# Cross-attention on one core: another hand-written order for the same 2281 operations, 127 of them on another engine

## The chip, the cores and the metric

The kernel runs on one core of a Trainium2 chip. A core has five engines with a queue of instructions each: TensorE (PE, matrix products), VectorE (DVE), ScalarE (ACT), GpSimd (POOL) and SyncE (SP, which only starts transfers). An engine works through its own queue strictly in order; an instruction waits on semaphores that other engines and transfers raise. Sixteen DMA engines move data between HBM and the on-chip memory (SBUF). The metric is the device time of one execution in microseconds (us); lower is better.

## The reference, cut to what matters

```python
# x (2, 2048, 640), ctx (2, 128, 384); H = 640, 8 heads of 80; T = 4 adapter tokens
enc, ca = ctx[:, :124], ctx[:, 124:]
query = x @ Wq
hs    = mha(query, enc @ Wk, enc @ Wv)            # 2048 x 124 scores per head
ca_q1 = einsum('btc,th->bch', ca, Wq_ca)[:, linspace(0, 383, 2048).astype(int)]
ca_hs1 = mha(ca_q1, x, x)                         # 384 distinct rows x 2048 keys per head
ca_hs2 = mha(ca_hs1 @ Wq, ca @ Wk_ca, ca @ Wv_ca) # 2048 x 4 scores per head
out = (hs + ca_hs2) @ Wout + b_out + x
```

All data is 32-bit float. The 2048 rows of `ca_q1` hold only 384 different ones, so the second attention is worked out for 384 rows and spread to the output rows at the end by indirect transfers that add.

## The kernel before, in words

**Stages.** The image rows of the two batch elements are cut into tiles of 128 rows (`xz`, `xi`, `x_more`, `last_rows` are buffers of such rows) and into 16 units of 256 rows (numbers 0 to 15 in names like `sc_5_0`, `po_15_1`). At the start the kernel loads x and the weights and turns them with TensorE transposes (`pt_x`, `pt_wq`, `pt_ctx`). `pq` products make the queries; `s`, `ea`, `acc` are scores, exponentials and sums of the adapter attention over the image (DVE takes a maximum `mx` of each block of scores, ACT the exponential `ea`, PE sums it into `acc`); `sc`, `m`, `p`, `eb`, `pT`, `ph` are scores, maxima, exponentials, transposed probabilities and results of the text attention; `po` is the product with Wout, whose pieces DVE adds to `x_more` or `last_rows`, whence they are stored. GpSimd adds the adapter's share `o` with one indirect transfer for a 128-row tile (line 2351).

**What sets the order.** The program is written by a small planner, the class `Desk`. Each stage is a Python generator that yields operations (`Do`); an operation has a set of engines that may run it. `Desk.run` (line 351) takes, of all operations that are ready to be written, the one with the lowest number in the table `TURNS` (line 85), and that number modulo six names the engine (PE, ACT, DVE, POOL, SP, or none). So `TURNS` alone fixes both the order of every queue and which engine does a copy, a sum or a store; each instruction is pinned in that order (`pin`, line 378). Lines 396, 405 and 410 issue the matrix products and transposes, line 427 all operations of DVE, ACT and POOL, line 447 the plain transfers, line 1363 a second kind of transfer for `xi`.

**Transfers.** ACT starts the loads of Wq, SP nearly all others, and both start stores. Wq comes in five chunks: two whole ones, two in halves of 64 rows, the fifth in five pieces of 16 or 32 rows (`chunk` and `last` in `first_loads`, line 667). The same generator then issues, on SP, four tiles `xz` of x, `wqca_sb`, `ctx_sb`, and the weights `w_kca` and `w_k` (128 partitions x 3 x 640 words, 983 KB each):

```python
yield Do("SP", lambda: dma(ctx_sb, enc.rearrange("b t c -> t b c"), 1.6), [], marks=["ctx"])
kca = yield load_w("kca", Wk_ca, after=[])
k = yield load_w("k", Wk, after=[])
```

In the built program the transfers of SP and ACT share eight completion semaphores, `DMAHW0` to `DMAHW7`, and a transfer that takes one of them first waits until the transfer that had it before has landed. The planner's own model has eight open transfers for each engine (`SLOTS`, line 74, `transfer`, line 450).

Of the kernel before, what the change touches and what calls it, by code (L numbers as in the profile page):

```python
# [65 lines left out]
class Desk:  # L66
# [19 lines left out]
        ".1": [995], ".2": [44, 59, 60, 84, 96, 108, 114, 120, 126, 132, 150, 174, 198, 210, 234, 978], ".3": [608],  # L86
        ".4": [5, 52, 76, 82, 94, 106, 352, 412, 442], ".4.1": [37, 67, 169, 241, 265], ".5": [468, 499, 534, 547,
        558, 584, 590], ".6": [11, 17, 144, 162, 204, 222, 258, 294, 300, 329], ".6.1": [140], ".6.2": [188],
        ".6.3": [218], ".6.4": [284], ".6.5": [157], ".6.6": [194], ".6.7": [229], ".6.8": [253], ".6.9": [278],
        ".6.10": [314], ".6.11": [319], ".7": [290, 510, 530, 1058], ".8": [23, 29, 35, 180, 246, 270, 306, 360,  # L90
        384, 396, 420, 426, 456, 486, 540, 576, 636, 726, 792, 803], ".8.1": [404], ".8.2": [416], ".8.3": [518],
        ".8.4": [703], ".8.5": [935, 1003, 1064, 1069, 1334], ".8.5.1": [1174], ".8.5.2": [1258], ".8.5.3": [1301],
        ".8.5.4": [1307, 1372, 1529, 1531, 1541, 1597], ".8.5.5": [1426], ".8.5.6": [1414], ".8.5.7": [1481],
        ".8.5.8": [1619, 1660, 1781, 1783, 1937, 1975], ".9": [368, 377, 450, 474, 485, 522, 564, 575, 618, 624,
        635, 672, 708, 762, 786], ".9.1": [464], ".9.2": [493], ".9.3": [553], ".9.4": [596], ".9.5": [643], ".9.6":
        [650], ".9.7": [685], ".9.8": [770], ".9.9": [812], ".9.10": [817], ".10": [605, 678, 716, 734, 828, 848,
        858, 919, 926, 936, 950, 972, 1088], ".11": [656, 744, 834, 912, 942, 960, 1025, 1031, 1039, 1052, 1084,
        1168, 1264, 1360, 1408, 1471], ".11.1": [782], ".11.2": [872], ".11.3": [956], ".11.4": [968], ".11.5":
        [1016], ".12": [1103, 1113, 1364], ".13": [760, 778, 1270], ".14": [724, 1176, 1214, 1308, 1328, 1416, 1441,
        1446, 1465, 1490, 1642, 1834, 1870, 1948, 2782, 4306, 5614, 6568], ".15": [694, 699, 984, 1032, 1242, 1272,  # L100
        1343], ".15.1": [1076], ".15.2": [1094], ".15.3": [1279], ".15.4": [1315], ".16": [1509], ".17": [335, 1104,
        1141, 1147, 1157, 1160, 1183, 1196, 1220, 1285, 1352], ".17.1": [1544, 1588, 1592, 1612, 1715, 1721, 2596,
        2830, 3832, 4780], ".18": [341, 1139], ".19": [809, 2663], ".20": [346, 358, 382, 394, 436, 448, 508, 616,
        664, 671, 752, 824, 842, 854, 866], ".21": [881, 1794, 1843, 1861, 1877, 1880, 1897, 1958, 1982, 2029,
        2078], ".21.1": [1886, 1912, 2084, 2116, 2219, 2225, 2362, 2734, 3028, 5020], ".22": [893, 2201], ".23":
        [2171, 3683], ".24": [887, 1128, 1200, 1320, 1344, 1392, 1458, 1482, 1644, 1704, 1740, 1836, 1926, 1950,
        2016, 2154, 2165], ".24.1": [1573], ".24.2": [1495], ".24.3": [1807], ".24.4": [1963], ".24.5": [2213, 2239,
# [2484 lines left out]
```

## Time and profile before

| | |
|---|---|
| time, median of 3 runs | 572.53 us (572.38 to 573.33) |
| profiled execution, span | 571.3 us |
| PE busy | 563.6 us (99%), 8069 products |
| DVE busy | 394.4 us (69%) |
| ACT busy | 286.7 us (50%) |
| POOL busy | 159.8 us (28%) |
| granted TensorE clock | full in all 40 slices |

The profile is of one execution. Its span is counted from the first record, so it is a little shorter than the time; the median of the runs lies 1.2 us above it. A busy PE is not a PE at its full pace: records of products overlap and their ends are modelled, so a PE that waits a little for each product can look busy.

### The profile page before, as it was taken

How to read it: one execution, taken by the hardware profiler on the slowest of the kernel's cores; microseconds unless marked ns; L12 is line 12 of the kernel's file. 1: busy time of each engine (PE TensorE's matmuls, PEld its weight loads, DVE VectorE, ACT ScalarE, POOL GpSimd, SP SyncE). 2: the span in 40 equal slices, each digit the busy share in tenths (PEclk: the TensorE clock that was granted, in tenths of full speed). 3: DMA queues.
4: the chain of work that ended last, by engine and by line, in shares of the span. 5: the costliest groups of instructions: out<-in, count | busy, mean ns of one | idle time of the engine just before them, and what ended most of it. 6: DMA issues, size and time to landing. Idle time of an engine off the chain costs nothing.

```text
span 571.3 us, 18875 instructions
## 1 busy us (share of the span) xinstructions
PE 563.6 (99%) x8069; PEld 310.0 (54%) x8069; DVE 394.4 (69%) x659; ACT 286.7 (50%) x806; POOL 159.8 (28%) x213
## 2 busy tenths in 40 slices
PE   9999999999999999999999999999999999999997
PEld 8885335455555455466554554554555554445553
DVE  4366999999998577458999999998332213544443
ACT  2021355645566899899876654524554664100000
POOL 9102041114440731100004350531203053045152
PEclk9999999999999999999999999999999999999999
DMA  8998576965968977446746969977476587799888
GB/s 246 211 248 126 139 161 157 172 179 139 211 212 153 215 182 211 146 126 198 233 158 203 316 180 319 245 217 230 96 263 120 164 206 223 248 211 213 258 156 237
DMA packets 145691, 113.21 MB, mean 198 GB/s; under 512 B 82548, under 2 KB 116980, under 8 KB 145608
## 3 DMA queue, kind: packets, MB, share of 16 engines
q1 hardware_dynamic: 137000, 95.10, 60.0%
q0 software_dynamic: 5632, 10.69, 11.7%
q10 hardware_dynamic: 2976, 6.23, 3.2%
q8 instruction: 63, 1.03, 0.8%
q14 instruction: 20, 0.16, 0.1%
HBM read 71.60 MB, written 40.39 MB: 196 GB/s over the span
## 4 chain that ended last, share of the span: by engine, by line
PE 92%; DVE 3%; ACT 3%; DMA 1%; issue 1%; SPq 0%; ACTq 0%; DVEq 0%
PE po L405 27%; PE pq L405 24%; PE sc L396 7%; PE acc L396 7%; PE s L396 7%; PE ph L396 6%; PE pq L396 4%; PE pyz L396 2%; ACT ea L427 2%; DVE mx L427 2%; PE pv L396 1%; PE pk L396 1%; DMA xz<-in_x_dram 1%; ACT p L427 1%; PE pt_wq L410 1%
## 5 line engine op out<-in xcount | busy, mean ns | idle before, releaser
L427 ACT ACTIVATE p<-sc,m 128x124 f32<-128x124 f32 x256 | 90.1, 381 | 43.4 <-DVE m L427 38.4
L427 DVE TENSOR_REDUCE mx<-s 128x4 f32<-128x2048 f32 x48 | 109.0, 2271 | 1.9 <-PE s L396 1.9
L427 ACT ACTIVATE ea<-s 128x2048 f32<-128x2048 f32 x48 | 90.5, 1884 | 31.4 <-PE s L396 30.9
L405 PE MATMUL po<-wout_sums,hs 128*32 128x320 f32 x1024 | 78.5, 434 | 0.1
L405 PE MATMUL po<-wout_sb,hs 128*32 128x320 f32 x928 | 72.4, 433 | 0.0
L427 POOL TENSOR_TENSOR p<-p,r 128x992 f32<-128x992 f32 x17 | 31.4, 1847 | 130.9 <-DVE r L427 130.9
L405 PE MATMUL pq<-xt,wq_sb 128*32 128x256 f32 (+1 forms) x928 | 66.4, 418 | 0.0
L427 DVE TENSOR_TENSOR last_rows<-last_rows,po 128x320 f32<-128x320 f32 x60 | 28.1, 480 | 44.0 <-PE po L405 43.9
L427 ACT ACTIVATION_READ_ACCUMULATOR p<-sc,m 128x1 f32 x256 | 57.0, 223 | 0.0
L427 DVE TENSOR_TENSOR x_more<-x_more,po 128x320 f32<-128x320 f32 x68 | 32.4, 481 | 34.5 <-PE po L405 32.5
L405 PEld LDWEIGHTS po<-wout_sums,hs 128*32 128x32 f32 x1024 | 33.4, 110 | 32.7 <-issue 2.8
L427 DVE TENSOR_REDUCE m<-sc 128x4 f32<-128x496 f32 x64 | 40.8, 663 | 14.1 <-PE sc L396 14.0
L396 PE MATMUL acc<-ea,y_sb 128*32 128x384 f32 (+2 forms) x768 | 50.2, 382 | 0.2 <-ACT ea L427 0.2
L396 PE MATMUL ph<-pT,vpad 128*32 128x256 f32 x768 | 47.9, 381 | 0.0
L405 PEld LDWEIGHTS po<-wout_sb,hs 128*32 128x32 f32 x928 | 30.1, 110 | 28.2 <-issue 1.6
L2351 POOL DMA_INDIRECT x_more<-o,query x17 | 26.6, 1563 | 67.0 <-DVE x_more L427 31.1
L405 PEld LDWEIGHTS pq<-xt,wq_sb 128*32 128x32 f32 x928 | 27.7, 110 | 28.0 <-issue 13.4
L427 ACT COPY hs<-ph 128x512 f32<-128x512 f32 (+1 forms) x25 | 13.4, 551 | 57.7 <-PE ph L396 57.7
L427 DVE STREAM_TRANSPOSE eb<-p 128x1024 f32<-128x1024 f32 x32 | 39.4, 1233 | 1.2 <-POOL p L427 1.1
L396 PEld LDWEIGHTS sc<-kmain,q 64*128 64x128 f32 x512 | 31.8, 187 | 12.6 <-issue 5.8
L427 POOL TENSOR_TENSOR hs<-hs 128x256 f32<-128x256 f32 x31 | 28.9, 1019 | 33.9 <-ACT hs L427 25.6
L396 PE MATMUL sc<-kmain,q 64*128 64x124 f32 x512 | 38.0, 285 | 0.0
(219 smaller groups left out, 835.0 us busy)
## 6 DMA issues: line engine op xcount, KB each, us to landing
kept<-eb SPq DMA_DIRECT2D x32, 512.0 KB
pT<-kept SPq DMA_DIRECT2D x16, 1024.0 KB
landing<-away SPq DMA_DIRECT2D x15, 512.0 KB
xi<-in_x_dram SPq DMA_DIRECT2D x56, 128.0 KB
x_more<-in_x_dram SPq DMA_DIRECT2D x17, 320.0 KB
last_rows<-in_x_dram SPq DMA_DIRECT2D x15, 320.0 KB
y<-yt SPq DMA_DIRECT2D x16, 256.0 KB
y_sb<-y SPq DMA_DIRECT2D x32, 128.0 KB
```

What stands on the lines that cost most here:

```text
L396: self.pin(self.nc.tensor.matmul(out, lhsT, rhs, **kw))
L405: self.pin(self.nc.tensor.matmul(out[j : j + 32], lhsT[:, j : j + 32], rhs, **kw))
L410: self.pin(self.nc.tensor.transpose(out, in_, ident))
L427: self.pin(getattr(engine, what)(*args, **kw))
L2351: desk.pin(nc.gpsimd.indirect_dma_start(out=t, out_offset=None, in_=o2_of[b], in_offset=bass.IndirectOffsetOnAxis(ap=query[:, st : st + 1] ...
```

## The change

Only the table `TURNS` differs. It has the same 617 entries and 2281 numbers. By the number modulo six, 127 operations change engine: 30 from DVE to ACT, 29 from DVE to POOL, 26 from ACT to DVE, 14 from POOL to DVE, 12 from ACT to SP, 7 from ACT to POOL, 6 from SP to ACT and 3 from POOL to ACT. In instructions: five normalising products `p<-p,r` go from ACT (eight instructions of 124 words each) to POOL (one of 992 words); of the sums `hs<-hs` DVE has 21 instead of 33 and POOL 43 instead of 31; DVE copies nine results `ph` instead of twelve and five queries instead of eight, ACT four and three more; ACT issues nine stores instead of fifteen. PE does the same products in another order. The file is eight lines longer, so lines 396, 427, 447 are lines 404, 435, 455 in the changed kernel.

```diff
     TURNS = {
...
-        ".4": [5, 52, 76, 82, 94, 106, 352, 412, 442], ".4.1": [37, 67, 169, 241, 265], ".5": [468, 499, 534, 547,
...
+        ".4": [5, 76, 88, 166, 214, 226, 310, 322, 334], ".4.1": [115, 133, 247, 253, 265], ".5": [336, 392,
...
```

The two entries shown belong to `first_loads`: `.4` are SP's loads (the last two numbers are `w_kca` and `w_k`), `.4.1` the five chunks of Wq on ACT.

**First place: the first loads.** SP's queue from its second row, before the change (names are as above; `xi_1` is the second group of rows of x; a number behind a name tells buffers apart; in brackets the semaphores that the row waits for):

```order
L447 DMA wqca_sb<-in_L_xattn_Wq_ca_dram 4x640
L447 DMA ctx_sb<-in_ctx_dram 128x2x384
L447 DMA xi_1_275<-in_x_dram 32x32x32 [waits DMAHW4_49,DMAHW3_49,DMAHW5_49,DMAHW1_49,DMAHW6_49,DVE_49,PE_49]
L1363 DMA xi_1_275<-in_x_dram 32x32x32 [waits DMAHW2_49]
L447 DMA xi_1_275<-in_x_dram 32x16x16 [waits DMAHW3_49]
L447 DMA xi_1_275<-in_x_dram 32x16x16 [waits DMAHW4_49]
L447 DMA xi_1_275<-in_x_dram 32x32x32 [waits DMAHW5_49]
L1363 DMA xi_1_275<-in_x_dram 32x32x32 [waits DMAHW6_49]
L447 DMA w_kca<-in_L_xattn_Wk_ca_dram 128x3x640 [waits DMAHW7_49]
L447 DMA xi_1_275<-in_x_dram 32x16x32 [waits DMAHW0_49]
L447 DMA w_k<-in_L_xattn_Wk_dram 128x3x640 [waits DMAHW1_49]
```

The same queue in the changed kernel:

```order
L455 DMA wqca_sb<-in_L_xattn_Wq_ca_dram 4x640
L455 DMA ctx_sb<-in_ctx_dram 128x2x384
L455 DMA w_kca<-in_L_xattn_Wk_ca_dram 128x3x640 [waits DMAHW0_49]
L455 DMA w_k<-in_L_xattn_Wk_dram 128x3x640 [waits DMAHW1_49]
L455 DMA xi_1_295<-in_x_dram 32x32x32 [waits DMAHW4_49,DMAHW5_49,DMAHW3_49,DMAHW7_49,DVE_49,PE_49]
L1371 DMA xi_1_295<-in_x_dram 32x32x32 [waits DMAHW3_49]
```

`w_kca` and `w_k` stand right behind `ctx_sb`, ahead of all loads of `xi`; they wait only for the first chunk of Wq (`DMAHW0`) and the first tile of x (`DMAHW1`).

ACT's queue at the same place, before:

```order
L447 DMA wq_sb<-in_L_xattn_Wq_dram 64x640 [waits DMAHW3_49]
L427 COPY xt_0_164<-pt_x_1_223 128x384 [waits PE_49]
L447 DMA wq_sb<-in_L_xattn_Wq_dram 16x640 [waits DMAHW4_49]
L447 DMA wq_sb<-in_L_xattn_Wq_dram 16x640 [waits DMAHW5_49]
L447 DMA wq_sb<-in_L_xattn_Wq_dram 32x640 [waits DMAHW7_49]
L447 DMA wq_sb<-in_L_xattn_Wq_dram 32x640 [waits DMAHW0_49]
L447 DMA wq_sb<-in_L_xattn_Wq_dram 32x640 [waits DMAHW1_49]
L427 COPY xt_0_164<-pt_x_1_266 128x2x128 [waits PE_49]
```

and in the changed kernel:

```order
L455 DMA wq_sb<-in_L_xattn_Wq_dram 64x640 [waits DMAHW5_49]
L455 DMA wq_sb<-in_L_xattn_Wq_dram 16x640 [waits DMAHW6_49]
L455 DMA wq_sb<-in_L_xattn_Wq_dram 16x640 [waits DMAHW0_49]
L455 DMA wq_sb<-in_L_xattn_Wq_dram 32x640 [waits DMAHW1_49]
L455 DMA wq_sb<-in_L_xattn_Wq_dram 32x640 [waits DMAHW2_49]
L455 DMA wq_sb<-in_L_xattn_Wq_dram 32x640 [waits DMAHW4_49]
L435 COPY q_208<-pq_0_209 128x2x256 [waits PE_49]
```

The fifth chunk's pieces are the rows of 16 and 32 lines. Before, the last two waited for the two halves of the third chunk, which had `DMAHW0` and `DMAHW1` last. Now the second piece waits for a count of two landings on `DMAHW0`, the second of which is `w_kca`, and the third for two landings on `DMAHW1`, the second of which is `w_k`; the last two stand behind them. The product that needs the fifth chunk, on PE, waits for all of its pieces in both kernels.

**Second place: ACT in the adapter's scores of the first batch element**, from the eighth to the twelfth block of its second half (`ea_1_7` to `ea_1_11`). Before:

```order
L427 ACTIVATE ea_1_7_3487<-s_0_1_7_3478 128x2048
L427 CAST zop_0_3210<-zb_0_1_3441 128x512
L427 CAST rests<-landing 128x512
L427 ACTIVATE ea_1_8_3548<-s_0_1_8_3539 128x2048
L427 ACTIVATE p_830,r_4_3535<-sc_4_0_3515,m_4_0_3533 128x4x31 x4
L427 ACTIVATE ea_1_9_3595<-s_0_1_9_3586 128x2048
L427 ACTIVATE p_830,r_4_3535<-sc_4_1_3516,m_4_1_3534 128x4x31 x4
L427 ACTIVATE ea_1_10_3634<-s_0_1_10_3625 128x2048
L427 CAST zop_1_3403<-zb_1_0_3578 128x512
L427 ACTIVATE p_831,r_5_3659<-sc_5_0_3639,m_5_0_3657 128x4x31 x4
L427 ACTIVATE ea_1_11_3695<-s_0_1_11_3686 128x2048
```

In the changed kernel:

```order
L435 ACTIVATE ea_1_7_3683<-s_0_1_7_3674 128x2048
L435 ACTIVATE p_813,r_5_3666<-sc_5_0_3646,m_5_0_3664 128x4x31 x4
L435 ACTIVATE p_813,r_5_3666<-sc_5_1_3647,m_5_1_3665 128x4x31 x4
L435 CAST zop_0_3626<-zb_0_1_3706 128x512
L435 ACTIVATE ea_1_8_3769<-s_0_1_8_3760 128x2048
L435 CAST zop_2_3770<-zb_2_0_3771 128x512
L435 CAST x_sums<-pq_4_3697 128x256
L435 ACTIVATE ea_1_9_3807<-s_0_1_9_3798 128x2048
L435 CAST wq_sums<-pq_4_3697 128x256
L435 ACTIVATE ea_1_10_3856<-s_0_1_10_3847 128x2048
L435 CAST zop_1_3821<-zb_1_0_3822 128x512
L435 ACTIVATE ea_1_11_3897<-s_0_1_11_3888 128x2048
```

From `ea_1_8` to `ea_1_11` the three groups of four text exponentials are gone; casts stand there.

**Third place: the last stores on SP.** Before, the queue ended with

```order
L447 DMA out_dram<-last_rows 128x640 [waits DMASW3_49,DVE_49]
L447 DMA out_dram<-last_rows 128x640 [waits DMAHW0_49,DMASW6_49,DVE_49]
L447 DMA out_dram<-x_more 128x320 [waits DMAHW5_49,DMASW1_49,DVE_49]
L447 DMA out_dram<-x_more 128x320 [waits DMAHW7_49,DMASW2_49,DVE_49]
L2587 UNCONDITIONAL_BRANCH
```

and it now ends with

```order
L455 DMA out_dram<-x_more 128x640 [waits DMAHW3_49,DMASW7_49]
L455 DMA out_dram<-last_rows 128x320 [waits DMAHW5_49,DMASW1_49,DVE_49]
L455 DMA out_dram<-last_rows 128x320 [waits DMAHW6_49,DVE_49]
L455 DMA out_dram<-last_rows 128x640 [waits DMAHW7_49,DMASW6_49]
L2595 UNCONDITIONAL_BRANCH
```

A whole store of 128 x 640 words has moved behind the halves of the last tile.

418 rows, old and new, of the table TURNS are left out of this document.

## The prediction

> **What bounds the kernel now.** I read the page's shares first, then the chain of waits.
>
> ```profile
> PE 563.6 (99%) x8069; PEld 310.0 (54%) x8069; DVE 394.4 (69%) x659; ACT 286.7 (50%) x806; POOL 159.8 (28%) x213
> PE 92%; DVE 3%; ACT 3%; DMA 1%; issue 1%; SPq 0%; ACTq 0%; DVEq 0%
> ```
>
> PE is busy nearly all the time and carries 92% of the chain. The products are the same after the change, so it can gain only where PE waits for others, and lose where it comes to wait. The 6% of DVE and ACT on the chain are 34 us, but PE works during most of that, so I looked where these pieces lie and what PE did there (the chain, then windows cut at its pieces, then PE's groups in the first of them):
>
> ```profile
> 264.76 1.78 ACT ea L427
> 267.79 1.90 ACT ea L427
> 269.68 0.63 ACT p L427 x4
> 274.55 1.95 ACT ea L427
> 300.77 2.24 DVE mx L427
> 307.23 2.20 DVE mx L427
> 310.94 2.17 DVE mx L427
> ```
>
> ```profile
> 264.14:276.55 12.41, 11.84 (x192) 7.33 (x189) 10.18 (x16) 12.41 (x31) 0.33 (x1) 1.00 0.73 233
> 300.07:313.15 13.08, 11.97 (x162) 5.78 (x162) 13.08 (x14) 7.83 (x30) 5.89 (x4) 1.00 0.62 192
> 327.22:334.24 7.02, 6.88 (x108) 3.90 (x109) 7.02 (x7) 3.45 (x13) 4.44 (x5) 1.00 0.66 194
> ```
>
> A window's columns are its length, then busy time and count for PE, weight loads, DVE, ACT and POOL, the clock, the DMA share and GB/s. In the first window ACT never pauses (12.41 of 12.41), in the other two DVE never does. PE has 0.57, 1.11 and 0.14 us with no record at all; what it loses between records that look joined comes from its own pace elsewhere:
>
> ```profile
> L396 PE MATMUL acc<-ea,y_sb 128*32 128x256 f32 (+2 forms) x64 | 4.3, 384 | 0.2 <-ACT ea L427 0.2
> L396 PE MATMUL sc<-kmain,q 64*128 64x124 f32 x32 | 2.7, 287 | 0.0
> L396 PE MATMUL s<-cop,zop 32*128 32x128 f32 (+2 forms) x32 | 2.1, 340 | 0.2 <-ACT ea L427 0.2
> L405 PE MATMUL pq<-x_sums,wq_sb 128*32 128x256 f32 x32 | 1.9, 379 | 0.0
> L396 PE MATMUL sc<-krest,rests 64*128 64x124 f32 x16 | 1.5, 279 | 0.0
> L405 PE MATMUL pq<-xt,wq_sb 128*32 128x256 f32 x16 | 1.1, 385 | 0.0
> ```
>
> ```profile
> 222.46 0.47 PE s L396 x8
> 257.50 1.00 PE acc L396 x16
> 259.36 0.86 PE acc L396 x16
> 284.81 5.32 PE pq L405 x96
> 290.56 1.49 PE sc L396 x24
> ```
>
> The lower fence is the chain where PE itself sets the pace: 0.059 us for one `s`, 0.054 to 0.062 for `acc`, 0.055 for `pq`, 0.062 for `sc`. The first window's 64, 48, 32 and 48 of these are 3.7 + 3.0 + 1.9 + 2.7 = 11.3 us in 12.41: some 1.1 us lost, of which 0.57 shows as idle. So real loss is about twice the visible one: 1.1 + 2.2 + 0.3 = 3.6 us in these windows. ACT's and DVE's other chain pieces (some 34 us less the 32.5 us of these three windows) leave little more; 4 us in all is my reading, 6 the most, 0 the least that can be won there.
>
> **The start.** The first loads were read in order of time, then the bytes moved in 40 bins of 0.7 us from 0 to 28 us:
>
> ```profile
> 8.62 2.94 ACTq L447 DMA_DIRECT2D wq_sb<-in_L_xattn_Wq_dram  x5
> 12.18 5.34 PE L396 MATMUL pq<-xt,wq_sb 128*128 128x256 f32 x24
> 12.38 0.37 ACT L427 COPY xt<-pt_x 128x256 f32<-128x256 f32 x1 [3.31 <-DMA wq_sb<-in_L_xattn_Wq_dram]
> 14.84 1.31 DVE L427 COPY wq<-wq_sb 128x320 f32<-128x320 f32 x2 [1.99 <-DMA wq_sb<-in_L_xattn_Wq_dram]
> 16.33 1.59 SPq L447 DMA_DIRECT2D w_kca<-in_L_xattn_Wk_ca_dram  x1
> 18.50 0.49 SPq L447 DMA_DIRECT2D w_k<-in_L_xattn_Wk_dram  x1
> ```
>
> ```profile
> 12.34 9.07 PE pq L396 x42
> ```
>
> ```profile
> GB/s 0 0 51 172 377 406 417 406 410 413 383 383 220 249 241 245 222 169 99 59 158 88 165 92 130 194 114 111 274 377 421 316 265 355 391 349 201 118 117 66
> ```
>
> Wq's fifth chunk was all in by 14.84, when DVE could copy from it. A product of this stage takes 9.07/42 = 0.216 us, so the fifth chunk's (the last eight of the 24 from 12.18) began at 12.18 + 16 x 0.216 = 15.6: just in time.
>
> **The change part by part.**
>
> *1. The wait for Wq's fifth chunk.* The second and third piece now share completion semaphores with `w_kca` and `w_k` and are issued only when these have landed; ACT's queue is in order, so the fourth and fifth stand behind. Behind them, too, wait ACT's copies of `q` and `xt`, DVE's two copies `wq` and what DVE has behind those, but PE comes to a stand first, at the fifth chunk's product. When does `w_k` land? The ten busy bins up to 8.4 us carried 3418 x 0.7 = 2393 KB. Up to and with `w_k` the changed queues move 1311 (x) + 655 + 655 (Wq's four large chunks) + 393 (`ctx`) + 1966 + some 50 = 5030 KB, so 2640 KB more. At the best bin, 417 GB/s, that takes 6.3 us; at 344, the mean of the eight bins from 19.6 us in which these same weights were moved, 7.7 us; at 235, the mean of the five bins from 8.4 us with Wq's half chunks, 11.2 us. With half a us to land: 15.2, 16.6 or 20.1. I take 16.6, because long rows will be in flight throughout. After that three pieces are issued (about 1 us; five took 2.94 with waits) and the last one lands; from the end of issuing (11.56) to DVE's start was 3.3 us before, in a crowd, so 2 to 3.3 here and I take 2.4. The chunk is complete at 20.0 (18.2 to 24.4).
>
> The Trainium skill, DMA: Bandwidth & Descriptors, Specifications, gives a core about 358 GB/s of HBM. The bins of 406 to 417 here are above it, so the measurement decides; by the page the best case would be 1.1 us later.
>
> PE gets there earlier than before: by its queue three idle products (`unread`) and two transposes that stood ahead now stand behind, 3 x 0.216 (two records of half the length each) + 2 x 0.108 = 0.86 us, so at about 14.8. It stands for **5.2 us** (3.4 to 9.6). Nothing covers it: every later product on PE is queued behind this one.
>
> The same page's section on queues, rings and completion order has SP's and ACT's transfers on separate rings that an engine serves in turn. By that rule the third and fourth chunk get their share beside the big loads, and only the issue of the fifth is late: the same sum.
>
> *2. What stands later on PE:* the **0.86 us** just named, and seven more changes of tile shape in its queue (268 for 261). One costs what a group pays on entry: `acc` 1.00 behind another shape against 0.86 behind its own, 0.14, so **0.9 us** (0 to 1.5).
>
> *3. Work moved off the crowded engines.*
>
> ```profile
> L427 ACT ACTIVATE p<-p,r 128x124 f32<-128x124 f32 x72 | 21.8, 388 | 8.6 <-DVE r L427 8.6
> L427 POOL TENSOR_TENSOR p<-p,r 128x992 f32<-128x992 f32 x17 | 31.4, 1847 | 130.9 <-DVE r L427 130.9
> L427 POOL TENSOR_TENSOR hs<-hs 128x256 f32<-128x256 f32 x31 | 28.9, 1019 | 33.9 <-ACT hs L427 25.6 <-DVE hs L427 7.8
> L427 DVE TENSOR_TENSOR hs<-hs 128x256 f32<-128x256 f32 x33 | 16.2, 497 | 5.5 <-POOL hs L427 5.2
> ```
>
> Forty `p<-p,r` fewer relieve ACT by 40 x 0.30 = 12 us, twelve sums fewer relieve DVE by 12 x 0.49 = 6 us; POOL gets 5 x 1.85 + 12 x 0.93 = 20 us more on 160, and has room. In the ACT-bound window three groups of four exponentials leave (269.68: 0.63 us on the chain for one, about 1.3 on ACT), 4 us against casts of 0.5: ACT no longer bounds there. On DVE the relief is thinner. I take the whole **-4.0 us**; both ends are 0 (the waits only move, POOL's slow products being the next to be late) and -6.
>
> *4. The end.*
>
> ```profile
> 565.85 1.29 PE L405 MATMUL po<-wout_sb,hs 128*32 128x320 f32 x16
> 566.08 1.97 SPq L447 DMA_DIRECT2D out_dram<-x_more  x2
> 567.18 0.34 ACTq L447 DMA_DIRECT2D out_dram<-x_more  x1
> ```
>
> The span ends 4.1 us behind PE's last product (567.14). A 328 KB store now stands behind the last half stores on SP. At 400 GB/s and one more issue (0.34) that is **+0.6 us** (0 to 1.0), unhidden, as nothing follows.
>
> **The sum:** 5.2 + 0.86 + 0.9 - 4.0 + 0.6 = +3.5 us on the profiled 571.3, 574.8; the median of the runs is 1.2 above the span, so **576.0 us**. With part 1 at its ends 574.2 and 580.4, part 3 adds 4 or takes 2.
>
> **The rivals.** (a) *Faster: the small waits are larger than I priced.* My pace comes from stretches where DVE and ACT also worked; if a quarter of their 34 us on the chain is PE's loss, 8.5 us are to be won, and with the start at its best (3.4) the sum is 3.4 + 2.35 - 8.5 = -2.8: 569.8. For it: real loss was twice the visible one where I could count. Against: most of the run after 400 us is like the window below, with no neighbour near its limit, where nothing is to be won.
>
> ```profile
> 400.00:425.00 25.00, 25.00 (x416) 12.90 (x408) 9.45 (x20) 13.82 (x10) 4.05 (x3) 1.00 0.54 152
> ```
>
> (b) *They cancel:* stall 3.4, gain 6: -0.2, 572.3; so also if the pieces do not go out in the order I read and PE's order wins little. (c) *Slower still: POOL becomes the late one.*
>
> ```profile
> L427 DVE STREAM_TRANSPOSE eb<-p 128x1024 f32<-128x1024 f32 x32 | 39.4, 1233 | 1.2 <-POOL p L427 1.1
> ```
>
> A multiply takes 1.85 us there, and what little DVE's transposes `eb` wait for is it; DVE's queue is in order, so a late multiply holds the maxima `mx` and with them PE. It decides once POOL's extra 20 us fall into DVE-bound stretches; then part 3 is 0: 571.3 + 7.5 + 1.2 = 580.0. Against: POOL was idle 130.9 us waiting for `r` ahead of these products.
>
> **How the numbers follow.** Forecast 0.45, (a) 0.24, (b) 0.16, (c) 0.15. A change under 0.2% (1.1 us) can't be told from none here. The forecast and (c) are slower but for the tail of the former's own range (573 to 579): slower 0.57; (a) and a little of (b) faster 0.25; same 0.18. The range to hold 8 in 10 runs from (a) to (c): 570.0 to 580.0.
>
> **What would show it.** In the changed profile: ACT's queue with Wq transfers issued at 15 to 18 us rather than all before 11.6, each behind a landing weight; PE idle, put down to a transfer of `wq_sb`, for 3 us or more between 13 and 22 us; SP's `w_kca` issued near 5. For part 3: in the adapter's scores of both elements, fewer chain pieces of ACT `ea` and DVE `mx`, and hardly any idle PE. For part 4: a span that ends 4.8 us behind PE's last product rather than 4.1. No idle PE before 25 us would refute part 1, and then about 570.9 is due; chain pieces of POOL in the first element's scores would speak for (c).

## The result: slower by 19 us, where 3.5 were forecast

The changed kernel took 591.72 us (median; 589.92 to 595.05) against 572.6 us before (now four runs): a ratio of 1.0335, 95% interval 1.0303 to 1.0368. The direction was forecast (576.0, range 570.0 to 580.0), the size was not: 19.1 us were lost, more than five times the 3.5 us of the forecast. The profiled execution after is the fastest of its runs, with a span of 588.1 us, 16.8 us above the span before; the other runs lie up to 5 us above it.

The profile after, shares first (busy time by engine, then the chain of waits by engine):

```profile
PE 568.9 (97%) x8069; PEld 308.3 (52%) x8069; DVE 388.8 (66%) x640; ACT 278.6 (47%) x771; POOL 180.7 (31%) x232
PE 65%; DVE 16%; DMA 8%; ACT 4%; issue 3%; SPq 3%; POOL 0%; ACTq 0%; DVEq 0%
PEclk8899999999999999999999999999999999999999
```

DVE and ACT have less to do and POOL more, as the change says. But PE's share of the chain fell from 92% to 65%: 16% is now DVE's and 8% are transfers. And the granted clock, full in all slices before, is short of full in the first two.

The main ones of PE's waits, from the same profile (us in total, times, longest):

```profile
PE pq L404 <- DMA wq_sb<-in_L_xattn_Wq_dram: 4.8, 2, 3.5
PE po L413 <- DVE last_rows L435: 2.1, 1, 2.1
PE pt_x L418 <- DVE xt L435: 1.6, 1, 1.6
PE po L413 <- DVE x_more L435: 1.5, 1, 1.5
PE po L413 <- DVE wout_sums L435: 1.0, 1, 1.0
```

The first and the third are at the start, 6.4 us, with 0.6 more for a transfer of `xz`; the other three, 4.6 us, are at two places in the middle. To place the loss in time I worked out a lag from PE's records: a product takes at least 0.83 ns for each column of its moving operand (products of 256 columns follow one another at 0.216 us, those of 128 at 0.109; products on parts of the array share the time), and a change of tile shape takes what it took in smooth stretches. The sum of these over PE's queue, up to a product, is the time at which PE would get there unhindered; the real time less that is the lag. It is the same measure for any order of the same products. The unhindered total comes to 545.2 us before and 546.1 after. These prices are worked out, not recorded: slightly other ones move the entries in the middle of the table by up to some 2 us, where a stand falls near the edge of a stretch; the loss before 40 us and the one at the end hold to a few tenths. The lag in us at these points of PE's work:

```
unhindered time       40   180   240   300   340   400   540   end
before               5.0   8.4  10.1  13.6  16.5  17.7  21.2  21.5
after               15.6  18.6  22.9  24.3  29.2  33.4  36.7  37.1
lost more by after +10.6  -0.4  +2.6  -2.1  +2.0  +3.0  -0.2  +0.1
```

The last row is what each stretch adds to the difference: 15.6 in all, and 0.9 of unhindered time, 16.5 of the span's 16.8. Two thirds are lost before 40 us. Between 240 and 300 us the change loses 2.1 us less than the kernel before, and from 300 to 340 it loses 2.0 more; the edge at 300 lies right at one of its stands. Over the whole of 240 to 340 us, in which the three windows of the prediction lie, nothing is won. Between 180 and 240 and between 340 and 400 it loses another 5.6 us.

**The start after.** The chain of waits passes through it (start, length, what):

```profile
5.13 14.30 DMA w_k<-in_L_xattn_Wk_dram
...
19.46 0.32 ACTq L455
...
20.29 3.42 DMA wq_sb<-in_L_xattn_Wq_dram
...
23.95 2.38 PE pq L404 x8
```

This is the mechanism of the prediction's first term, link by link: SP's `w_k`, issued at 5.13, lands at 19.43; only then does ACT issue the third piece of Wq's fifth chunk, then the others; the last, issued at 20.29, is in 3.42 us later, and PE's product starts at 23.95. Forecast were 16.6 for `w_k` and 20.0 for the product. PE's own rows there:

```profile
8.36 0.90 PE L418 MATMUL pt_x<-ident,first_rows 128*128 128x128 f32 x3 [1.57 <-DVE xt L435]
...
18.53 1.97 PE L404 MATMUL pq<-xt,wq_sb 128*128 128x256 f32 x8 [1.33 <-DMA wq_sb<-in_L_xattn_Wq_dram]
...
23.95 2.38 PE L404 MATMUL pq<-xt,wq_sb 128*128 128x256 f32 x8 [3.45 <-DMA wq_sb<-in_L_xattn_Wq_dram]
```

The fourth chunk was late too (18.53). And PE is slow when it does work (windows: length, PE's busy time and count, granted clock, DMA share, GB/s; after, then one of before, where all of these had 1.00):

```profile
8.00:10.00 2.00, 1.64 (x8) 0.57 1.02 384
10.00:12.00 2.00, 2.00 (x13) 0.57 1.06 348
...
24.00:26.00 2.00, 2.00 (x8) 0.84 0.62 95
26.00:28.00 2.00, 2.00 (x8) 0.50 0.59 85
28.00:30.00 2.00, 2.00 (x12) 0.81 0.93 128
```

```profile
26.00:28.00 2.00, 2.00 (x12) 1.00 1.23 99
```

Twice PE is granted about half its clock for some 4 us behind a stand: from 8.36, when it works again, to 12 that is 3.6 x 0.43 = 1.6 us lost, and 2 x (0.16 + 0.50 + 0.19) = 1.7 from 24 to 30. Not every stand costs clock: behind the one of 1.33 us at 18.53 the windows show 1.00. With the stands, 0.6 + 1.6 + 4.8, this makes 10.3 of the 10.6 us.

**The middle after**, in order of time around the second of two stands of the output product:

```profile
321.25 2.42 DVE L435 TENSOR_TENSOR prod<-prod 128x288 f32<-128x288 f32 x2
321.44 2.06 POOL L435 TENSOR_TENSOR p<-p,r 128x992 f32<-128x992 f32 x1
...
325.66 1.82 PE L413 MATMUL po<-wout_sb,hs 128*32 128x320 f32 x24 [1.03 <-DVE wout_sums L435]
...
328.44 0.48 DVE L435 TENSOR_TENSOR x_more<-x_more,po 128x320 f32<-128x320 f32 x1
...
328.98 1.23 PEld L413 LDWEIGHTS po<-wout_sb,hs 128*32 128x32 f32 x24 [2.08 <-DVE x_more L435]
```

PE's next output product needs the bank that DVE's addition to `x_more` empties, and that addition stands in DVE's queue behind the copy `wout_sums`, maxima `m`, the second softmax and `zop`. DVE hardly pauses there (it is busy 13.4 of the 14 us from 316 to 330); PE does.

### The profile page after: what moved, and what is told of

The parts are those of the page before. It is cut to its first block, busy times and chain, and to the rows that moved or that the text cites. A ratio compares the mean times of both kernels' runs of the same rounds, so it can differ in the third digit from the quotient of the medians.

```text
span 588.1 us, 18831 instructions
## 1 busy us (share of the span) xinstructions
PE 568.9 (97%) x8069; PEld 308.3 (52%) x8069; DVE 388.8 (66%) x640; ACT 278.6 (47%) x771; POOL 180.7 (31%) x232
## 3 DMA queue, kind: packets, MB, share of 16 engines
q0 software_dynamic: 5632, 10.69, 10.7%
q8 instruction: 63, 1.03, 0.7%
## 4 chain that ended last, share of the span: by engine, by line
PE 65%; DVE 16%; DMA 8%; ACT 4%; issue 3%; SPq 3%; POOL 0%; ACTq 0%; DVEq 0%
PE po L413 24%; PE pq L413 9%; PE acc L404 7%; DVE mx L435 6%; PE ph L404 6%; PE s L404 5%; PE sc L404 4%; PE pq L404 3%; DMA w_k<-in_L_xattn_Wk_dram 2%; SPq L455 2%; PE pyz L404 2%; ACT p L435 2%; DVE eb L435 2%; DVE m L435 2%; DVE xt L435 1%
## 5 line engine op out<-in xcount | busy, mean ns | idle before, releaser
L435 POOL TENSOR_TENSOR p<-p,r 128x992 f32<-128x992 f32 x22 | 42.3, 1924 | 161.8 <-DVE r L435 161.8
L413 PE MATMUL po<-wout_sb,hs 128*32 128x320 f32 x960 | 74.1, 434 | 2.5 <-DVE x_more L435 1.5
L435 POOL TENSOR_TENSOR hs<-hs 128x256 f32<-128x256 f32 x43 | 34.1, 819 | 89.0 <-ACT hs L435 44.7
L435 DVE TENSOR_TENSOR last_rows<-last_rows,po 128x320 f32<-128x320 f32 x64 | 30.4, 484 | 46.5 <-PE po L413 46.0
L435 DVE TENSOR_TENSOR x_more<-x_more,po 128x320 f32<-128x320 f32 x64 | 30.2, 481 | 42.8 <-PE po L413 42.2
L435 DVE TENSOR_REDUCE m<-sc 128x4 f32<-128x496 f32 x64 | 39.9, 664 | 16.6 <-PE sc L404 16.6
L413 PEld LDWEIGHTS po<-wout_sums,hs 128*32 128x32 f32 x1024 | 31.5, 110 | 35.2 <-DVE last_rows L435 4.2
L435 ACT COPY hs<-ph 128x512 f32<-128x512 f32 (+1 forms) x29 | 15.6, 555 | 68.0 <-PE ph L404 67.9
L404 PE MATMUL ph<-pT,vpad 128*32 128x256 f32 x768 | 46.4, 381 | 0.1
L435 ACT COPY q<-pq 128x512 f32<-128x512 f32 x27 | 16.1, 596 | 38.7 <-DMA xi<-in_x_dram 17.9
```

What stands on the lines that cost most here:

```text
L404: self.pin(self.nc.tensor.matmul(out, lhsT, rhs, **kw))
L413: self.pin(self.nc.tensor.matmul(out[j : j + 32], lhsT[:, j : j + 32], rhs, **kw))
L435: self.pin(getattr(engine, what)(*args, **kw))
```

## The experiments

The edits are edits of the table of turns; one also raises the number of idle products. An edited table can name an operation that cannot yet be written, so in the edited kernels `Desk.run` takes the lowest number among those that can:

```diff
-            op = min((op for q in self.queue.values() for op in q), key=turn)
+            op = min((op for q in self.queue.values() for op in q if self.ready(op) is not None), key=turn)
```

Where an order is changed over at some point, the point is a time of PE's unhindered work; all operations ahead of it in the first order come first, the rest follows in the second order.

### The start alone

*The change's order and engines up to 40 us of PE's work, then those of before:*

```diff
-before up to the end
+after up to 40 us of PE's work, before from there to the end
```

> The changed order for the first 40 us of PE's work, the order of before for all that is left. Theory (the start alone costs some 11 us): 582 to 586. Rival (later waits follow from the late start): 587 to 592.

Measured 584.48 us (583.35 to 586.03), 1.0200 [1.0174, 1.0225] of before: 11.5 us. The lag is 16.0 at 40 us and 32.2 at the end, against 5.0 and 21.5: what is lost at the start is lost for good, and nothing is added later. This is the time that the theory gave. PE's waits name the same transfer:

```profile
PE pq L405 <- DMA wq_sb<-in_L_xattn_Wq_dram: 5.2, 2, 3.7
```

*Before, with nothing but the two loads moved* (SP's queue):

```diff
 DMA ctx_sb<-in_ctx_dram 128x2x384
+DMA w_kca<-in_L_xattn_Wk_ca_dram 128x3x640
+DMA w_k<-in_L_xattn_Wk_dram 128x3x640
 DMA xi_1<-in_x_dram 32x32x32
...
-DMA w_kca<-in_L_xattn_Wk_ca_dram 128x3x640
 DMA xi_1<-in_x_dram 32x16x32
-DMA w_k<-in_L_xattn_Wk_dram 128x3x640
```

> The kernel before with one edit: SP's loads of w_kca and w_k stand right behind ctx_sb, ahead of the loads of xi, and by the semaphores the third piece of Wq's fifth chunk waits for w_k to land. Nothing else is moved; PE's order is the one of before. Theory (these two loads are what makes PE's start late): nearly the 11.9 us that the whole start of the change cost, 581 to 585 us, with PE standing for wq_sb between 13 and 24 us. Rival (PE's own new order at the start, in which it also stands from 5.8 to 8.4 us and is then given less than its full clock, carries half of it or more): 574 to 578.

Measured 583.34 us (582.91 to 584.1), 1.0174 [1.0157, 1.0191]: 9.9 of the 11.5 us. Two rows in SP's queue do nearly all of the start's damage, with PE's order left as it was. PE's rows (the releaser in the last one shares a semaphore with the piece of Wq and is named in its place) and one of the three windows from 24 to 30 us, which all have a clock of 0.50:

```profile
14.91 1.97 PE L405 MATMUL pq<-xt,wq_sb 128*128 128x256 f32 x8 [2.45 <-DMA wq_sb<-in_L_xattn_Wq_dram]
17.50 1.97 PE L405 MATMUL pq<-xt,wq_sb 128*128 128x256 f32 x8 [0.63 <-DMA wq_sb<-in_L_xattn_Wq_dram]
24.11 3.75 PE L405 MATMUL pq<-xt,wq_sb 128*128 128x256 f32 x8 [4.65 <-DMA xi<-in_x_dram]
```

```profile
26.00:28.00 2.00, 2.00 (x6) 0.50 0.99 137
```

Stands of 7.7 us and 2 x 1.5 = 3 us of withheld clock make 10.7; the lag at 40 us is 11.0 above before. The rival, that PE's own order carries half, falls.

*The changed kernel, with the two loads back among those of `xi`* (SP's queue):

```diff
 DMA ctx_sb<-in_ctx_dram 128x2x384
+DMA xi_1<-in_x_dram (six pieces)
 DMA w_kca<-in_L_xattn_Wk_ca_dram 128x3x640
+DMA xi_1<-in_x_dram 32x16x32
 DMA w_k<-in_L_xattn_Wk_dram 128x3x640
-DMA xi_1<-in_x_dram (the same seven pieces)
```

> The changed order, with only the loads of w_kca and w_k moved back to their old places among the loads of xi. Theory (the first loads cost the start some 10 us because Wq's last pieces wait for these two loads and because the rest of Wq shares the DMA engines with them): the fifth chunk is complete by about 15 us, PE's wait for Wq is under 1 us, and the time falls by 7 to 10 us to 582 to 585. Rival (the start is late because of PE's and DVE's own order, or because the clock was withheld): the wait moves elsewhere, and the time falls by less than 3 us.

Measured 598.08 us (596.76 to 599.24), 1.0429 [1.0405, 1.0454]: slower than the change itself, and both expectations missed. The start did get better (lag 9.7 at 40 us instead of 15.6), but then

```profile
PE pw L404 <- issue: 5.7, 1, 5.7
PE po L413 <- DVE last_rows L435: 5.4, 2, 3.4
```

the gain went into a wait at 63 us that PE's lateness had covered, and into another near the end.

*The change, with PE kept busy while it waits:* 22 idle products (two records of half the length each, 4.7 us in all) ahead of the products of the fourth and fifth chunk. They write to a bank that nobody reads.

```diff
 MATMUL pq_1<-xt,wq_sb 128x256 x2
+MATMUL unread<-zeros 128x128 x6
 MATMUL pq_0<-xt,wq_sb 128x256 x2
 MATMUL pq_1<-xt,wq_sb 128x256 x2
+MATMUL unread<-zeros 128x128 x16
 MATMUL pq_0<-xt,wq_sb 128x256 x2
```

> The changed order with 22 more idle products on PE: 6 ahead of the fourth chunk's product and 16 ahead of the fifth's, about 4.8 us of work at full clock inside waits of 1.3 and 3.6 us. Theory (PE's standing still lowers the clock granted to it for some microseconds afterwards): the clock from 24 to 30 us is 1.00 instead of 0.50 to 0.84, and the time falls by 1 to 2.5 us although PE does more. Rival (the clock is lower there for another reason): no lower time, or 0 to 1.5 us more.

Measured 591.07 us (590.17 to 594.44), 1.0320 [1.0280, 1.0360]: the same as the change. But the clock is a clear answer, in the same windows as above:

```profile
8.00:10.00 2.00, 1.56 (x8) 0.55 1.01 382
...
26.00:28.00 2.00, 2.00 (x13) 1.00 1.04 141
```

The theory on the clock holds, its gain in time did not come: with PE kept at work the clock behind the wait is full (1.00 in all three windows from 24 to 30 us); ahead of it, where nothing was added, it is short as before. At 60 us of PE's own work this left it 1.1 us earlier (lag 10.4, and 4.7 us of added products, against 16.2), and later waits took that back.

### Semaphores or crowding?

The prediction let the fifth chunk be late because its issue waits. The run with two loads moved does not tell that from plain crowding by 1966 KB. So ACT's issues of Wq were put ahead, which by the order in which the semaphores are dealt out leaves no piece of Wq waiting for `w_kca` or `w_k`; first in before alone, as a base (ACT's queue):

```diff
 DMA wq_sb<-in_L_xattn_Wq_dram 128x640 x2
+DMA wq_sb<-in_L_xattn_Wq_dram 64x640 x4
 COPY xt<-pt_x 128x256
-DMA wq_sb<-in_L_xattn_Wq_dram 64x640 x2
 COPY xt<-pt_x 128x256
-DMA wq_sb<-in_L_xattn_Wq_dram 64x640 x2
-COPY xt<-pt_x_1 128x384
 DMA wq_sb<-in_L_xattn_Wq_dram 16x640 x2
 DMA wq_sb<-in_L_xattn_Wq_dram 32x640 x3
+COPY xt<-pt_x_1 128x384
```

> Before with ACT's issues of Wq moved: the halves of the third and fourth chunk right behind the first two chunks, ahead of ACT's first copy xt, and the five pieces behind the second copy. Nothing else is moved. It is the base for the next run. Both theories: within 2 us of before, 572 to 575, since Wq was not waited for in before.

Measured 577.44 us (575.89 to 578.43), 1.0075 [1.0053, 1.0098]: 4.5 us, more than the 2 allowed. ACT's queue is in order, so its first copy `xt` now waits behind Wq's issues; PE stands for it for 3.0 us, and is given 0.58 of its clock from 8 to 12 us. That base with the two loads early:

```diff
 (ACT's queue as in the base)
 (SP's queue as in the run with the two loads alone)
```

> The same order of ACT's issues, and w_kca and w_k early as in the run with these loads alone moved. In this order no piece of Wq shares a semaphore with w_kca or w_k, so none waits for them to land; the two loads are still in flight beside Wq. Theory 1 (the semaphores: the fifth chunk is late because its issue waits for w_k): nearly all of the 9.9 us that the early loads cost is gone, 573 to 577. Theory 2 (crowding: 1966 KB more in flight make every chunk of Wq late, whatever is issued when): 579 to 584.

Measured 578.15 us (577.89 to 578.51), 1.0097 [1.0080, 1.0113]: 0.7 us above its base where the same two rows had cost 9.9. The time lies between the two ranges; the step from the base speaks for theory 1. But the transfers say that the total flatters it (KB each, at 1024 bytes, and median us from issue to landing; the base first, then with the loads early):

```profile
wq_sb<-in_L_xattn_Wq_dram ACTq DMA_DIRECT2D x2, 40.0 KB, 2.5
```

```profile
w_k<-in_L_xattn_Wk_dram SPq DMA_DIRECT2D x1, 960.0 KB, 12.0
...
wq_sb<-in_L_xattn_Wq_dram ACTq DMA_DIRECT2D x2, 40.0 KB, 5.4
```

Pieces that wait for nothing still take 5.4 us instead of 2.5. PE's product of the fifth chunk:

```profile
21.02 1.97 PE L405 MATMUL pq<-xt,wq_sb 128*128 128x256 f32 x8 [0.97 <-issue]
```

It starts at 21.02, after a stand of 0.97 us. It costs little because PE comes late to it anyway: the base had already lost 4.5 us ahead of it. A PE on time, at 15.6 as before, would have stood for some 5 us. So of the way from 15.6 to 23.95 some 5 us are crowding and some 3 the shared semaphores; the split is a rough estimate. The pieces are issued later in this base (12.1) than before (8.6), and SP issues `w_kca` and `w_k` later too, at 8.62 and 9.04 instead of the 4.85 and 5.27 of the run with these loads alone, so that four chunks of Wq were ahead of them. The two causes are not separated by these runs.

*The same edit in the changed kernel* (four half chunks ahead of ACT's first copy `xt`; the five pieces stay behind it):

```diff
 DMA wq_sb<-in_L_xattn_Wq_dram 128x640 x2
+DMA wq_sb<-in_L_xattn_Wq_dram 64x640 x4
 COPY xt<-pt_x_0 128x256
-DMA wq_sb<-in_L_xattn_Wq_dram 64x640 x4
 DMA wq_sb<-in_L_xattn_Wq_dram 16x640 x2
```

> The changed kernel with ACT's halves of Wq right behind the first two chunks; the five pieces stay behind its first copy xt, and wait for no landing of w_kca or w_k. Theory 1: the start no longer costs 11 but 2 to 5 us; but the run with the change's start replaced by that of before has shown that PE, when early, is then held at 60 us for blk_v, and the tail of the change is uneven, so 583 to 592 in all, with the lag of PE at 40 us 5 us or more below that of the change. Theory 2: 588 to 596, with the stand for Wq as long as before the edit.

Measured 593.13 us (587.43 to 593.35), 1.0323 [1.0270, 1.0375]. The lag at 40 us is 10.1 instead of 15.6, as theory 1 said, and no wait for `wq_sb` is left (here too the edit puts SP's issue of the two loads off, to 8.60 and 9.02 us), though the whole time is 1 us above the range that theory 1 gave (three runs lie at 593, one at 587). The rest gave it back: by 180 us it loses 5.9 where the change loses 3.0, and 5.4 more between 540 and 560 us of the profile's time. What happened there, in the chain of waits:

```profile
535.48 4.27 DMA out_dram<-x_more
...
539.76 9.72 DMA x_more<-in_x_dram
...
549.91 0.49 DVE last_rows L435
...
550.45 9.60 PE po L413 x113
```

SP's load of new rows into `x_more` waits until the store of the old ones has landed, then itself takes 9.72 us; DVE's addition to `last_rows` stands behind the one to `x_more`, and PE behind that. The profiled execution of the change has no such stand, but four kernels with its late part, this one among them, have one of 2 us or more there. It fits the spread of the change's own runs, 590 to 595, of which only the fastest has a profile; that it is their cause was not tested.

### The rest of the change without its start

*Before up to 40 us of PE's work, then the change:*

```diff
-after up to the end
+before up to 40 us of PE's work, after from there to the end
```

> The order of before for the operations of the first 40 us of PE's work, the changed order for all that is left. Theory (the start costs some 11 us, and the changed order later costs 4 to 6 us by itself): 576 to 581. Rival (the later waits only follow from the late start, and the later order by itself gains the 4 us that were forecast): 567 to 572.

Measured 593.50 us (592.62 to 594.87), 1.0360 [1.0338, 1.0382]. Both missed: the lag at 40 us is 5.1, so the start is mended, and the whole is no faster. PE loses 4.5 us between 60 and 80 us of the profile's time (a stand of 2.4 for `pw`, and withheld clock behind it) and 5.0 between 540 and 560. I thought that `pw` waits for the last pieces of Wout, and had SP issue them earlier:

```diff
 DMA xi_2<-in_x_dram 32x32x32
+DMA wout_sb<-in_L_xattn_Wout_dram 16x640 x8
+DMA bias<-in_L_xattn_b_out_dram 16x640
 DMA xi_2<-in_x_dram 32x16x32
...
-DMA wout_sb<-in_L_xattn_Wout_dram 16x640 x8
-DMA bias<-in_L_xattn_b_out_dram 16x640
```

> The order of before for the first 40 us of PE's work, then the changed order, as in an earlier run (593.5 us), but SP issues the eight small last pieces of Wout and the bias ahead of most loads of the third group of x. Theory (with the start early, PE comes to the product that needs these pieces before SP, which stands in order behind loads of x, has issued them: 2.9 us without work and 1.6 us at a lower clock): the wait at 60 us goes, 588 to 590. Rival (the wait is for something else, or the moved loads of x are missed instead): 592 to 596.

Measured 593.31 us (591.53 to 599.37), 1.0390 [1.0330, 1.0449]; the stand for `pw` grew to 7.4 us, so that reason falls. Its rows in order of time show the right one:

```profile
60.70 3.08 DVE L435 STREAM_TRANSPOSE xt<-xi 128x512 f32<-128x512 f32 x5 [7.49 <-DMA away<-first_rests]
...
67.33 0.40 DVE L435 TENSOR_SCALAR blk_v<-pt_vca,side 128x32 f32<-128x32 f32 x2
...
67.95 2.66 PE L404 MATMUL pw<-wout_sb,blk_v 128*32 128x320 f32 x10 [7.37 <-issue]
```

`pw` waits for `blk_v`, a DVE operation of 0.4 us. In DVE's queue it stands behind the transposes of the next rows `xi`, and DVE stood 7.49 us for those rows, whose loads the eight pieces had pushed back on SP. In the changed kernel PE's late start covers this wait. That is also where the repair of the two loads went.

*Before up to 170 us, then the change*, which leaves both out:

```diff
-after up to the end
+before up to 170 us of PE's work, after from there to the end
```

> The order and the engines of before for PE's first 170 us, then those of the change. The change's start is left out, and so is the place at 60 us at which its order made PE wait for blk_v. Theory (the change's order behind 180 us costs PE by itself: DVE's additions to x_more and last_rows stand behind maxima at 325 and 380 us, and PE's bank is freed late): 577 to 581, 5 to 8 us above before. Rival (those waits are a consequence of the late start, and the relief of the crowded engines is what is left): 567 to 571.

Measured 585.79 us (583.81 to 590.34), 1.0243 [1.0200, 1.0287], 12.4 us above before and above the range given. The rival falls with it: the waits are the same with an early start. The stands in the middle are the same to the tenth (the second one for `last_rows` lies near the end):

```profile
PE po L413 <- DVE last_rows L435: 3.5, 2, 2.1
PE po L413 <- DVE x_more L435: 1.5, 1, 1.5
PE po L413 <- DVE wout_sums L435: 1.0, 1, 1.0
```

The lag is 7.9 at 160 us, 14.7 at 200, 16.2 at 240, 17.6 at 300, 25.8 at 400 and 31.2 at the end. From 160 to 200 it loses 6.8 us where before loses 1.1; this is mostly the seam of two orders (stands of 1.4 and 0.9 us and a clock of 0.58 from 180 to 186 us, which the change does not have there), so this run prices the change too high there. From 240 to 300 it loses 1.4 us as the change does, 2.1 fewer than before; from 300 to 400 it loses 8.2, before 4.1, the change 9.1. Over 240 to 400 that is 9.6 us against 7.6 before: with an early start, too, nothing is won in the end.

*DVE operations put ahead in the changed kernel:* at 324 and 380 us the copy `wout_sums`, two additions to `x_more` and one to `last_rows` ahead of what they stood behind (in DVE's queue these are four operations that moved, not the five of the expectation).

```diff
+COPY wout_sums<-ph_4 128x256
 TENSOR_TENSOR prod<-prod 128x3x96
...
 TENSOR_REDUCE m_8_1<-sc_8_1 128x4
+TENSOR_TENSOR x_more<-x_more,po_0 128x320
 TENSOR_REDUCE r_0<-p_0 128x24
...
+TENSOR_TENSOR last_rows<-last_rows,po_2 128x320
 TENSOR_REDUCE mx<-s_1_2_1_1 128x4
-TENSOR_TENSOR last_rows<-last_rows,po_2 128x320
```

> The changed order with five DVE operations moved ahead at two places: at 324 us a copy of wout_sums ahead of the small products of the second softmax and two additions of po ahead of longer work, at 380 us one addition ahead of a maximum mx of 2.3 us. Theory (PE stands 1.0, 1.5 and 2.1 us there because what frees its output bank is queued behind long DVE work): 2 to 4 us less than the change, 587 to 590. Rival (DVE is the bound there whatever its order, so the waits move to the next maximum): 591 to 593.

Measured 596.05 us (594.06 to 598.02), 1.0403 [1.0367, 1.0439]. It did not help, and the time is above both ranges: from 300 to 400 us PE loses 9.9 us instead of 9.1. The stand for `wout_sums` is gone and the one at 380 us shorter, but the stand for `x_more` is longer than the change's 1.5:

```profile
PE po L413 <- DVE x_more L435: 2.4, 1, 2.4
```

So there the order of these operations is not the cause by itself. Nor is it the amount of DVE's work: from 320 to 380 us DVE is busy 95% of the time in the change and 96% before, where PE stood only 0.14 us. What makes the stands there stays open. Of the rest of this run's loss 4.6 us are the stand near the end, which the edit does not touch.

### Order and engines apart

*The change's order with the engines of before, and the reverse:*

```diff
-order of the change, engines of the change
+order of the change, engines of before
```

> The changed order of all operations, but each on the engine that it had before (the 127 moves undone, the order kept). Theory (the loss sits in the order, of loads and of DVE's queue, and the moves are worth less than 2 us either way): 589 to 595. Rival (the moves to POOL, whose products of two tensors hold up DVE, cost the time): 578 to 586.

```diff
-order of before, engines of before
+order of before, engines of the change
```

> The order of before, with the 127 operations on the engines of the change. Theory (as above): 571 to 576. Rival: 577 to 585.

Measured 634.13 (634.06 to 635.18) and 591.12 us (590.84 to 592.45): 1.1066 [1.1046, 1.1087] and 1.0324 [1.0301, 1.0347]. All four expectations were too low. The longest wait in each:

```profile
PE po L413 <- DVE x_more L435: 16.2, 3, 15.0
```

```profile
PE po L414 <- POOL hs L436: 7.1, 3, 5.0
```

Each half without the other is worse than or as bad as both together, so neither has a price of its own that could be read from these runs.

*Only the stretch with the relief taken from the change, in two lengths:*

```diff
-before up to the end
+before up to 240 us of PE's work, after from there to 316 (300), before from there to the end
```

> Before, with only the stretch between 240 and 316 us of PE's work in the order and on the engines of the change. Read from the two traces, PE lost 5.7 us between 240 and 320 us before and 2.8 after. Theory (the relief that the prediction reckoned with exists there, and is lost at other places): 569 to 571, some 2 to 3 us faster than before. Rival (the relief is only a wait put off: queues taken back at the end of the stretch are late there): 572 to 578.

> The same with the stretch cut at 300 us of PE's work, which leaves out the scores of the adapter's second half in the second element. Theory of the relief: between before and the run cut at 316, 570 to 572. Rival: 572 to 578, like the other.

Measured 658.20 us (654.68 to 659.31) and 645.89 us (642.96 to 648.32), 1.1488 [1.1469, 1.1507] and 1.1261 [1.1219, 1.1304]: far outside both expectations. In the first the lag grows from some 10 us at 240 us to over 90 at 420. A stretch of the one order does not find the queues there as it needs them. These two say nothing on the relief; the run from 170 us on does. No kernel here beats the one before.

## Why the prediction was wrong, point by point

**What bounds the kernel.** Right: PE's products are the same, and the loss is PE standing. What the reading left out is that PE can also lose clock after it has stood.

**Part 1, 5.2 us (3.4 to 9.6): the right mechanism, half the size.** Issue order, shared semaphores and the product that waits came as described, and the two loads alone reproduce the loss. The term, taken as what the start costs, measured 10.6 us. The stand for `wq_sb` by itself is 4.8 us, close to the 5.2, but that is luck: the chunk was complete 4 us later than taken (23.95 against 20.0), and PE was ready for it 5.7 us later than taken (20.5 against 14.8). Three steps failed.
- "I take 16.6, because long rows will be in flight throughout": `w_k` landed at 19.43. After, the bytes moved from 5 to 25 us in 40 bins of 0.5 us:

```profile
GB/s 405 364 369 410 397 396 369 367 384 415 404 394 364 230 257 313 271 303 308 270 306 298 269 241 213 135 74 67 82 118 134 188 148 72 277 191 133 25 72 77
```

 The rate holds near 400 up to 11.5 us and is 230 to 313 from there to 17. The mean from 8.5 to 16.5 is 322, not far below the 344 that were taken, so the 2640 KB reckoned up to `w_k` had been moved by about 16.7 us. But `w_k` landed 2.7 us after that, while the bins fell to 67 to 135 and loads of `xi`, issued from 15.13 on, were in flight beside it. The term that was mis-sized most is the half us to land, for which the prediction shows no row. What held the last rows of `w_k` back is open. From there to PE's product it took 4.5 us where 3.4 were taken.
- The third and fourth chunk "get their share" beside the big loads, so that no wait for them stood in the sum. The fourth was late, 1.33 us in the change and 3.1 us for both in the run with the loads alone. The prediction drew that from the Trainium skill, DMA: Bandwidth & Descriptors, in its section on queues, rings and completion order. The half chunks of 160 KB took 8.0 us (median) to land in the change, and pieces of 40 KB took 6.8:

```profile
wq_sb<-in_L_xattn_Wq_dram ACTq DMA_DIRECT2D x4, 160.0 KB, 8.0
wq_sb<-in_L_xattn_Wq_dram ACTq DMA_DIRECT2D x2, 40.0 KB, 6.8
```

 A separate ring did not make a small transfer quick.
- The clock, 3.3 us, and the 2.2 us for which PE stands ahead of 9 us (`pt_x` for DVE's `xt` and for `xz`), were put at nothing. Together with the fourth chunk's 1.33 us, these 2.2 us and the clock's first 1.6 us are why PE came to the fifth chunk so late. The prediction had seen that three idle products move away from there, and priced them as 0.86 us of work put off, not as a gap left open.

So the sum for the start should have read 4.8 (stands for Wq) + 2.2 (stands ahead of 9 us) + 3.3 (clock) = 10.3 us.

**Part 2, 0.9 us for tile shapes.** It is the difference of the two unhindered totals, which rest on the same price; no run tests it.

**Part 3, -4.0 us (0 to -6): no gain on balance, and a loss that it did not allow for.** The engines' totals moved much as reckoned: DVE by -5.6 us (forecast 6), ACT by -8.1 (12), POOL by +20.9 (20). But PE gained nothing from it: 2.1 us less are lost from 240 to 300 us, 2.0 more from 300 to 340, and another 5.6 from 180 to 240 and from 340 to 400. With small entries at the other places the net is a loss of 5.0 us. The failed steps are the whole relief of 4.0 us taken as PE's gain, and the upper end, "0 (the waits only move, ...)": work that goes to another engine in another order can make waits that were not there before. Here PE stands for DVE's additions that empty its output banks; why DVE comes late with them is not shown. Chain pieces of ACT `ea` are indeed fewer, but those of DVE `mx` are not: they went from 2% of the chain to 6%, and DVE's share as a whole from 3% to 16%. The 2.6 us between 180 and 240 are spread over waits under 1 us that no run took apart.

**Part 4, +0.6 us (0 to 1.0).** The span ends 588.1 - 583.7 = 4.4 us behind PE's last product, against 4.1 before: +0.3, and 4.8 was forecast. That it is near is not to the working's credit: 328 KB at 400 GB/s take 0.8 us and the issue 0.34, which makes 1.2 and not 0.6.

```profile
582.94 0.72 PE L413 MATMUL po<-wout_sb,wout_sums 128*32 128x320 f32 x8
```

**The span and the median.** 1.2 us were added; the median lies 3.6 above the profiled span, because the change's runs differ among themselves by 5 us where those before differed by 1.

**The rivals.** (a) and (b) fall: there is no gain. (c) had the right shape, part 3 lost to late queues, but PE waits for DVE and not for POOL (0% of the chain), and the loss has no floor at zero; whether POOL slows DVE there is looked at below. By the numbers above the sum should have read 10.6 + 0.9 + 5.0 + 0.3 = 16.8 us; 10.6 and 5.0 are read from the lag, so that this adds up is no proof of their causes.

**What would show it.** SP issued `w_kca` at 4.72, and ACT's Wq was held up as said, though to 20.7 rather than to 18 us; the stand of 3.45 us for `wq_sb` lies from 20.5 to 23.95 and not between 13 and 22:

```profile
6.84 13.89 ACTq L455 DMA_DIRECT2D wq_sb<-in_L_xattn_Wq_dram  x9
```

## What to carry to other kernels

A load that is moved ahead has two prices: the transfers that share its bandwidth land later, and so does whatever is issued on a completion semaphore that it now holds; add to them what PE may lose in clock after it has stood. A wait covered by an earlier lateness is not gone: repairs of the start showed two stands, at 60 and near 545 us, that the change's own profile does not have. And where work is moved between engines, an unchanged total is not the worst case: follow the small operations that free PE's banks, and see what they stand behind now.

## What the runs showed of the hardware

**The clock is withheld after some short stands.** In the changed kernel stands of 0.6 and 1.6 us, less than a microsecond of work apart, were followed by 0.57 of the clock from 8 to 12 us; a stand of 3.45 by 0.84, 0.50 and 0.81 from 24 to 30; in the base with Wq ahead one of 3.0 by 0.58. With idle products in the place of the stand of 3.45 the clock stayed at 1.00. Other stands of the changed kernel cost no clock: behind those of 1.33 us at 18.5, of 1.03 and 1.50 between 324 and 330, and of 2.06 at 382 us the windows show 1.00. The Trainium skill, TensorE: Matmul & The Clock Gate, Part 1, has the clock at half rate after an idle window of about 3.4 us. The half rate and the effect of idle products agree; the stands ahead of 9 us are shorter, each and together, and still cost clock. What tells them from the stands that cost none, these runs do not show.

**DVE slows beside POOL.** An operation on two tensors took several times as long where POOL's product ran beside it (before, then after; total us and mean ns of two):

```profile
L427 DVE TENSOR_TENSOR prod<-prod 128x144 f32<-128x144 f32 x2 | 0.6, 308 | 0.1
```

```profile
L435 DVE TENSOR_TENSOR prod<-prod 128x144 f32<-128x144 f32 x2 | 2.1, 1070 | 0.1
```

The two after differ: one, at 510.96, had nothing of POOL beside it and took 0.31 us as before. The other is the second operation in the row of 2.42 us at 321.25: it ran 1.83 us, from 321.84 to 323.67, beside POOL's multiply from 321.44 to 323.50, six times as long. In six other kernels here with the same middle it took 1.83 us beside the same multiply too. It stands in DVE's queue ahead of what PE waits for at 325.66 and 328.98, so the 1.5 us it loses are a candidate for these stands. The Trainium skill, SBUF — State Buffer, in its section on the two separate sides, has DVE and GpSimd share a pair of ports of which one holds the whole for an instruction. The rows fit that; no run moved POOL's product away to test it, or what it costs PE.
